# The last stage of a four-layer convolution kernel: two batches kept on chip, six loaded eight parts ahead

## The chip, the cores and the metric

The kernel runs on one core of a Trainium2 chip. The time is device microseconds of one execution; a measurement is the median of several executions. A profile is one further execution, recorded by the hardware profiler, whose span runs from its first to its last instruction. Engines are named as in the profile: PE (matrix multiply, with PEld for its weight loads), DVE (vector), ACT (scalar, activation functions), POOL (GpSimd), SP (the engine that issues most transfers). A queue's name with a q (SPq, ACTq) is the engine's instruction sequencer, which issues transfers.

## What is computed

The input is 8 batches of 128 channels and 64 x 64 points in float32. Four layers follow each other, each added to its own input after a group norm:

```
x = x + L0(gn(x))     # a state-space scan beside a 3x3 convolution
x = x + L1(gn(x))     # four directional passes over rows and columns
x = x + L2(gn(x))     # gated convolutions; its result is x3
x = x + L3(gn(x))     # deformable convolution, then a norm over the whole batch
```

Only the end of layer 3 matters here. With `out` the deformable convolution with its bias:

```
mu  = out.mean(axis=(0, 2, 3), keepdims=True)
var = out.var(axis=(0, 2, 3), keepdims=True)
out = (out - mu) * rsqrt(var + 1e-05)
out = out * gamma + beta
y   = x3 + where(out >= 0, out, 0.1 * out)
```

The mean and the variance run over all batches and points of a channel, so no point of the result can be finished before the last batch of the deformable convolution is done.

## The kernel before

A batch is 4096 columns on 128 partitions (channels); most work goes in parts of T = 512 columns, NCH = 8 to a batch. Layer 0 and the first half of layer 1 run first. Then a hand-written order (under `tc.manual_schedule()`, where instructions are issued in the order of the program) interleaves layer 1's second half, layer 2 and layer 3 in steps called ticks, N = 96 to a batch: at tick n, layer 3 works on batch n // N - 1 while layer 2 works on the batch after it. `spread(thread, steps, first, last)` divides a thread of small actions evenly over a range of ticks. The last 96 ticks hold layer 3 of batch 7 alone.

Layer 3 (class `Layer3`), a tick: `gather` (L1158) lets POOL issue three indirect DMAs, each fetching 128 rows of 512 values out of a table in HBM; ACT and DVE weigh and add the four corners (L1184, L1189, L1200 to L1202), PE turns the tile (`turn`, L1209), ACT copies it (L1219), PE multiplies with the weights (L1227). `biased` (L1233) adds the bias into a tile `o_out` of 512 columns, and `store` (L1242) has SP send it to `od` in HBM and DVE take its statistics (L1244). The gathered tiles are six buffers of the tag `got`. From tick L1R on, when layer 1 is done, they are ten slots of 1536 columns cut out of X instead, a tile of 4096 x 4 values for each partition (16384 columns) that held layer 1's state; `got` is then no longer used.

Layer 2 (class `Layer2`) writes x3 to `x3d` in HBM (L947) and uses tiles of the tags x2, xn2, t1, t3, tok (two buffers each) and x3h (one). For the last batch it ends some 14 ticks before tick 8N; its last transfers on SP are the table stores of L999.

The end stage is `finish` (L1255), called after the pools of layers 2 and 3 and the manual schedule are closed (L145). It derives mean and scale from the statistics (L1264 to L1268), opens a pool of four buffers, and goes over 32 parts of E = 1024 columns, four to a batch: SP loads x3 (L1274) and the stored result (L1276), DVE subtracts the mean and multiplies (L1277), ACT adds beta (L1278), DVE takes the larger of a value and its tenth (L1279), POOL adds x3 (L1280), ACT issues the store (L1281). A load into a buffer waits for the store out of it four parts earlier.

Of the kernel before, what the change touches and what calls it, by code (L numbers as in the profile page):

```python
# [10 lines left out]
F32 = mybir.dt.float32  # L11
I32 = mybir.dt.int32
AF = mybir.ActivationFunctionType
ALU = mybir.AluOpType
# [3 lines left out]
P = 128  # L18
B, C, H, W = 8, 128, 64, 64
HW = H * W  # L20
# [13 lines left out]
@with_exitstack  # L34
def conv_preact_kernel(ctx: ExitStack, tc: tile.TileContext, a: dict, out: bass.AP):
    nc = tc.nc
    x_in = a["x"].rearrange("b c h w -> b c (h w)")
    y_out = out.rearrange("b c h w -> b c (h w)")

    const = ctx.enter_context(tc.tile_pool(name="const", bufs=1))  # L40
    dram = ctx.enter_context(tc.tile_pool(name="dram", bufs=1, space=DRAM))


    ident = const.tile([P, P], F32, name="ident")
    make_identity(nc, ident)

    gmat = const.tile([P, P], F32, name="gmat")
    nc.gpsimd.memset(gmat, 0.25)
    gview = gmat.rearrange("p (g q) -> p g q", q=4)
    nc.gpsimd.affine_select(  # L50
        out=gview, in_=gview, pattern=[[-4, 32], [0, 4]], compare_op=ALU.is_ge,
        fill=0.0, base=0, channel_multiplier=1,
    )
    nc.gpsimd.affine_select(
        out=gview, in_=gview, pattern=[[4, 32], [0, 4]], compare_op=ALU.is_ge,
        fill=0.0, base=3, channel_multiplier=-1,
    )
    eps = const.tile([P, 1], F32, name="eps")
    nc.gpsimd.memset(eps, 1e-5)

    x1d = [dram.tile([C, HW], F32, name=f"x1d{b}") for b in range(B)]
    x2d = [dram.tile([C, HW], F32, name=f"x2d{b}") for b in range(B)]
    od = [dram.tile([C, HW], F32, name=f"od{b}") for b in range(B)]
    x3d = [dram.tile([C, HW], F32, name=f"x3d{b}") for b in range(B)]
    tables = [dram.tile([SIDE * SX, 2 * C], F32, name=f"table{b}") for b in range(B)]

    bcd = [dram.tile([P // 2, T], F32, name=f"bcd{i}") for i in range(2)]


    norm1 = const.tile([P, B, 2], F32, name="norm1")  # L70

    A, Z = range(NB2), range(NB2, B)
    norm2 = const.tile([P, B, 2], F32, name="norm2")
    st = const.tile([P, B * NCH, 6], F32, name="bn_st")
    xp = ctx.enter_context(tc.tile_pool(name="x", bufs=1))
    w1 = ctx.enter_context(tc.tile_pool(name="l1", bufs=2))
    X = xp.tile([P, HW, NB2], F32, name="X")
    layer0(tc, a, ident, gmat, x_in, x1d, bcd, norm1, Layer1First(tc, a, w1, x1d, norm1, X))  # L80

    with tc.tile_pool(name="l2w", bufs=1) as wp, tc.tile_pool(name="l2", bufs=2) as w2, tc.tile_pool(
        name="l3", bufs=2
    ) as w3, tc.tile_pool(name="l12ps", bufs=1, space=PSUM) as p2, tc.tile_pool(
        name="l3ps", bufs=2, space=PSUM
    ) as p3, tc.tile_pool(name="l3pr", bufs=1, space=PSUM) as pr, tc.manual_schedule():
        bank = p2.tile([P, T], F32, name="ps_l1")
        ps_l1 = bank[:, 0 : W * NB2].rearrange("p (w b) -> p w b", b=NB2)
        add = lambda tiles, ahead, b: residual(
            tc, w1, tiles, ahead, bank, gmat, eps, x1d, x2d, X, [(i, b[i]) for i in range(NB2)], norm2  # L90
        )


        first = add(lambda: w3.tile([P, Layer3.G3 * 4 * C], F32, tag="got", name="x_got", bufs=6), 4, A)
        for _ in range(NCH):
            next(first)
        two = Layer2(tc, a, ident, gmat, eps, x2d, x3d, tables, norm2, wp, w2, p2)
        three = Layer3(tc, a, ident, tables, od, st, wp, w3, p3, pr, X.rearrange("p n b -> p (n b)"))


        N = two.TICKS
        plans = {}
        for b in range(B):
            for when, what in two.plan(b).items():
                plans.setdefault(b * N + when, []).extend(what)
        ahead = []

        def spread(thread, steps, first, last):

            ahead.append((thread, steps, first, last))  # L110

        spread(first, 3 * NCH, 0, 12)
        for i in range(NB2):
            spread(load_x(tc, w1, x1d, norm1, X, i, Z[i]), NCH + 1, 4 * i, 4 * i + 4)

        n_l1 = 4 * (H - 1)
        L1A, L1Z = 18, NB2 * N - 22
        early = N - L1A
        L1R = L1Z + 40
        spread(add(lambda: w1.tile([P, T], F32, name="x1", bufs=3), 1, Z), NB2 * NCH, L1Z, L1R)  # L120
        step = propagate(tc, a, w1, ps_l1, X)
        next(step)
        taken = {}
        for n in range(min(plans), (B + 1) * N):
            b, i = n // N - 1, n % N
            if n < N:
                l1 = n >= L1A
            else:
                l1 = [(min(m, L1Z) - N) * (n_l1 - early) // (L1Z - N) for m in (n, n + 1)]
                l1 = l1[1] - l1[0]  # L130
            if l1:
                next(step)
            if b >= 0:
                three.tick(b, i, two.done, 1, n >= L1R)
            if l1:
                next(step)
            for f in plans.pop(n, ()):
                f()
            for k, (thread, steps, first, last) in enumerate(ahead):
                while first <= n and taken.get(k, 0) < -(-steps * min(n + 1 - first, last - first) // (last - first)):  # L140
                    taken[k] = taken.get(k, 0) + 1
                    next(thread)
        while three.late:
            three.tick()
    finish(tc, a, eps, od, x3d, y_out, st, const)  # L145


def layer0(tc, a, ident, gmat, x_in, x1d, bcd, norm1, layer1):
# [975 lines left out]
        return events  # L1124


class Layer3:


    PAIR, G3, WT = 2, 3, 4  # L1130

    def __init__(self, tc, a, ident, tables, od, st, wp, w2, pp, pr_pool, more):
        nc = self.nc = tc.nc
        self.ident, self.tables, self.od, self.st = ident, tables, od, st
        self.w2, self.pp, self.more = w2, pp, more
        self.dcn_w = wp.tile([P, KK, P], F32, name="dcn_w")
        nc.sync.dma_start(self.dcn_w, a["dcn_w"])
        self.dcn_b = wp.tile([P, 1], F32, name="dcn_b")
        nc.sync.dma_start(self.dcn_b, a["dcn_b"])

        self.prod = pr_pool.tile([P, 2, T], F32, name="prod")
        self.samp, self.blocks = {}, {}
        self.late = {}
        self.n = 0

# [86 lines left out]

    def biased(self, b, t0, ps):  # L1233
        nc, N2 = self.nc, self.PAIR * P
        if t0 % 4 == 0:
            self.out = self.w2.tile([P, T], F32, name="o_out")
        o = self.out[:, t0 % 4 * P : t0 % 4 * P + N2]
        nc.scalar.activation(o, ps, AF.Identity, bias=self.dcn_b)
        if t0 % 4:
            self.later(2, self.store, b, t0 // 4, self.out)  # L1240

    def store(self, b, g, out):  # L1242
        self.nc.sync.dma_start(self.od[b][:, g * T : (g + 1) * T], out)
        self.nc.vector.bn_stats(self.st[:, b * NCH + g, :], out)  # L1244

    def tick(self, b=None, i=0, done=None, halves=2, more=False):
# [5 lines left out]
        self.n += 1  # L1252


def finish(tc, a, eps, od, x3d, y_out, st, wp):  # L1255

    nc = tc.nc
    E = 2 * T
    gamma = wp.tile([P, 1], F32, name="gamma")
    nc.sync.dma_start(gamma, a["gamma"])  # L1260
    beta = wp.tile([P, 1], F32, name="beta")
    nc.sync.dma_start(beta, a["beta"])
    mv = wp.tile([P, 2], F32, name="bn_mv")
    nc.vector.bn_aggr(mv, st.rearrange("p a s -> p (a s)"))  # L1264
    sc = wp.tile([P, 1], F32, name="bn_sc")
    nc.scalar.activation(sc, mv[:, 1:2], AF.Sqrt, bias=eps)
    nc.vector.reciprocal(sc, sc)
    nc.vector.tensor_mul(sc, sc, gamma)  # L1268
    with tc.tile_pool(name="l3e", bufs=4) as ep:
        for b in range(B):  # L1270
            for g in range(HW // E):
                s = slice(g * E, (g + 1) * E)
                x3 = ep.tile([P, E], F32, name="x3")
                nc.sync.dma_start(x3, x3d[b][:, s])  # L1274
                v = ep.tile([P, E], F32, name="o_in")
                nc.sync.dma_start(v, od[b][:, s])  # L1276
                nc.vector.tensor_scalar(v, v, mv[:, 0:1], sc, ALU.subtract, ALU.mult)  # L1277
                nc.scalar.activation(v, v, AF.Identity, bias=beta)  # L1278
                nc.vector.scalar_tensor_tensor(v, v, 0.1, v, ALU.mult, ALU.max)  # L1279
                nc.gpsimd.tensor_add(x3, x3, v)  # L1280
                nc.scalar.dma_start(y_out[b][:, s], x3)  # L1281


def layouts(i):
# [55 lines left out]
```

## Time and profile before

| what | value |
|---|---|
| time, median of 3 (range) | 7452.86 us (7450.63 to 7460.66) |
| the profiled execution: its own time / its span | 7436.8 us / 7435.1 us |
| granted TensorE clock, mean | 0.857 |
| busy share of the span: PE, DVE, POOL, ACT | 76%, 65%, 55%, 45% |
| last 512 columns of layer 3 (start of L1244) | 7266.15 us |
| first operation of L1277 | 7272.93 us |
| last add of L1280 ends | 7427.85 us |
| moved from 7266 to 7436 | 50.62 MB, 298 GB/s on average |

The busy shares are averages over stages with different limits, so they say little on a stage of 169 us at the end of 7435; that stage has to be read on its own. In lists of groups and of single instructions, a row has the line, the engine, the operation, what is written and read, and the shapes; a bracket at the end says how long the engine had been idle and what ended that. In lists of waits, the columns are the total in us, how many waits, and the longest. "remote" is a releaser that the profile could not name. A row of a table by windows has the busy us of PE, PEld, DVE, ACT and POOL, each with its count, then the granted clock, the busy share of the DMA engines and GB/s.

The transfers of the end stage, issues with their size:

| transfer | issued by | count | KB each |
|---|---|---|---|
| x3 load (L1274) | SP | 32 | 512 |
| result load (L1276) | SP | 32 | 512 |
| output store (L1281) | ACT | 32 | 512 |

### The profile page before, as it was taken

To read this page: it belongs to the slowest core of one execution; us is meant where nothing else is said; L and a number is where in the kernel's file an instruction comes from. 1 tells how busy PE (TensorE), PEld (TensorE's weight loads), DVE (VectorE), ACT (ScalarE), POOL (GpSimd) and SP (SyncE) were. 2 spreads that over 40 slices of the span, in tenths; PEclk is the share of its full clock that TensorE was granted. 3 is DMA by queue.
4 is the path that set the end of the run, shared out by engine and by line. 5 is a ranking of instruction groups with operands and counts; after the bars stand their busy time and mean duration, and the time that the engine had idled before them with its cause. 6 is when DMAs were issued, how large, how long until landed. Compare 5 with 4: busy or idle time off the path is not lost.

```text
span 7435.1 us, 79753 instructions
## 1 busy us (share of the span) xinstructions
PE 5633.9 (76%) x25130; PEld 3374.0 (45%) x25130; DVE 4822.2 (65%) x6334; ACT 3349.0 (45%) x7610; POOL 4120.9 (55%) x3773
## 2 busy tenths in 40 slices
PE   6888888899999999779898988984556565554330
PEld 1222222255556556647676767762333333333220
DVE  4988889666666666230366666758767676776665
ACT  3555655433333332020255555554556565565552
POOL 3878778545545454000255555555666666666664
PEclk9888888799999999989999999996777677776665
DMA  1111111101100100130356666667677666666667
GB/s 57 43 58 54 57 56 53 42 29 34 32 30 30 31 20 18 59 124 24 96 180 188 189 183 180 192 187 243 211 217 219 208 212 209 211 212 201 187 182 272
DMA packets 360134, 935.09 MB, mean 126 GB/s; under 512 B 64168, under 2 KB 99248, under 8 KB 357664
## 3 DMA queue, kind: packets, MB, share of 16 engines
q0 software_dynamic: 184320, 604.13, 26.7%
q1 hardware_dynamic: 170784, 309.09, 12.8%
q10 hardware_dynamic: 4608, 16.78, 0.6%
q8 instruction: 200, 3.28, 0.2%
q14 instruction: 222, 1.82, 0.1%
HBM read 804.35 MB, written 125.40 MB: 125 GB/s over the span
## 4 chain that ended last, share of the span: by engine, by line
PE 56%; ACT 11%; issue 9%; DVE 9%; another core or an unknown queue 7%; DMA 4%; POOL 4%; SPq 0%; POOLq 0%; DVEq 0%; ACTq 0%
PE u_ps L739 13%; PE ps_l L739 11%; ACT X L1184 6%; PE u_ps L575 5%; PE ps_o L1227 5%; PE ps_c L484 3%; PE ps_t L900 3%; PE ps_y L629 3%; PE ps_s L1209 2%; PE ps_x L392 2%; DVE hb L610 2%; POOL hb L621 2%; PE ps_off L1017 2%; PE ps_t L926 1%
## 5 line engine op out<-in xcount | busy, mean ns | idle before, releaser
L1173 POOL DMA_INDIRECT X<-table,idx x1386 | 1317.9, 951 | 717.0 <-issue 276.6
L1173 POOL DMA_INDIRECT got<-table,idx x918 | 885.1, 964 | 1291.2 <-DVE idx L1078 529.6
L621 POOL TENSOR_TENSOR hb<-hb,bc 128x1024 f32<-128x1024 f32 x512 | 1207.1, 2358 | 47.0 <-POOL carry L616 4.5
L610 DVE TENSOR_TENSOR_SCAN hb<-da,carry,u_ps 128x512 f32<-128x512 f32 x896 | 1097.8, 1267 | 76.4 <-PE ps_y L629 19.8
L592 ACT ACTIVATE da<-dt_ps 128x1024 f32<-128x1024 f32 x512 | 524.8, 1025 | 1284.2 <-PE dt_ps L575 1087.4
L1184 ACT ACTIVATE X<-X,wgt 128x128 f32<-128x128 f32 x2772 | 867.5, 396 | 41.5 <-issue 37.7
L1227 PE MATMUL ps_o<-samp,dcn_w 128*128 128x256 f32 x2304 | 711.8, 455 | 182.9 <-issue 95.8
L1219 ACT COPY samp<-ps_s 128x384 f32<-128x384 f32 x768 | 362.9, 473 | 1043.9 <-remote 563.0
L575 PE MATMUL u_ps<-u,m_u 32*128 32x512 f32 x2048 | 652.3, 716 | 131.2 <-DVE hb L610 130.5
L599 DVE TENSOR_TENSOR u_ps<-u_ps,bc 128x1024 f32<-128x1024 f32 x512 | 625.8, 1222 | 191.2 <-PE dt_ps L575 173.9
L1209 PE MATMUL ps_s<-ident,X 128*128 128x128 f32 x1386 | 306.4, 344 | 576.2 <-ACT samp L1219 287.0
L575 PE MATMUL dt_ps<-dt,m_dt 32*128 32x512 f32 x2048 | 664.0, 728 | 31.5 <-ACT da L592 25.7
L1227 PEld LDWEIGHTS ps_o<-samp,dcn_w 128*128 128x128 f32 x2304 | 507.3, 231 | 309.4 <-issue 128.6
L747 DVE SCALAR_TENSOR_TENSOR X<-ps_l,X 128x256 f32<-128x256 f32 x252 | 106.6, 423 | 734.5 <-PE ps_l L739 553.6
L1200 DVE TENSOR_TENSOR prod<-prod,X 128x384 f32<-128x384 f32 x462 | 260.8, 565 | 480.0 <-ACT X L1184 320.5
L1184 ACT ACTIVATE got<-got,wgt 128x128 f32<-128x128 f32 x1836 | 570.3, 393 | 1.1 <-issue 1.1
L1209 PEld LDWEIGHTS ps_s<-ident,X 128*128 128x128 f32 x1386 | 206.1, 176 | 708.9 <-ACT samp L1219 330.5
L616 POOL COPY carry<-hb 128x2 f32<-128x2 f32 x512 | 111.4, 218 | 735.0 <-DVE hb L610 678.8
L1189 DVE TENSOR_TENSOR prod<-X,prod 128x768 f32<-128x768 f32 x462 | 444.5, 962 | 46.2 <-ACT prod L1156 27.6
L747 DVE SCALAR_TENSOR_TENSOR X<-u_ps,X 128x256 f32<-128x256 f32 x252 | 106.9, 424 | 562.7 <-PE u_ps L739 560.4
L900 PE MATMUL ps_t<-xn,w 128*128 128x512 f32 (+4 forms) x688 | 344.8, 656 | 66.5 <-issue 23.0
L575 PEld LDWEIGHTS u_ps<-u,m_u 32*128 32x128 f32 x2048 | 169.6, 202 | 483.6 <-DVE hb L610 282.2
(227 smaller groups left out, 10644.6 us busy)
## 6 DMA issues: line engine op xcount, KB each, us to landing
bc<-bcd SPq DMA_DIRECT2D x512, 64.0 KB
table<-tok SPq DMA_DIRECT2D x128, 256.0 KB
x<-x1d SPq DMA_DIRECT2D x96, 256.0 KB
X<-table,idx POOLq DMA_INDIRECT x1386
x<-x2d SPq DMA_DIRECT2D x48, 384.0 KB
x3h<-x3d SPq DMA_DIRECT2D x16, 1056.0 KB
x_st<-in_x SPq DMA_DIRECT2D x64, 256.0 KB
x_o<-in_x SPq DMA_DIRECT2D x64, 256.0 KB
```

The lines of the kernel that those rows point to most:

```text
L575: nc.tensor.matmul(ps[:, j, :], lhsT=mask[q, r].rearrange("p d n -> p (d n)"), rhs=S[c][src, h][q, :], start=True, stop=True,)
L592: nc.scalar.activation(da, steps[i]["dt"], AF.Exp)
L599: nc.vector.tensor_mul(st["bc"], st["bc"], s["bc", h][:, 0].unsqueeze(1).to_broadcast([P, 2, T]))
L610: nc.vector.tensor_tensor_scan(hb[:, j, :], st["da"][:, j, :], st["bc"][:, j, :], start, ALU.mult, ALU.add)
L621: nc.gpsimd.tensor_mul(hb, hb, S[c]["bc", h][:, 1].unsqueeze(1).to_broadcast([P, 2, T]))
L739: nc.tensor.matmul(ps[:, c0:c1, :], lhsT=w[:, k, :], rhs=v[:, prev, c0 + k - PAD : c1 + k - PAD, :], start=(k == PAD), stop=(k == K - 1),)
L900: nc.tensor.matmul(ps[:, o0 - a0 : o1 - a0, :], lhsT=self.w1[:, k, :], rhs=S["xn", g][:, i0 + o0 : i0 + o1, :], start=(k == 2), stop=(k == 4),
L1173: nc.gpsimd.indirect_dma_start(out=got[:, k, :, :].rearrange("p q c -> p (q c)"), out_offset=None, in_=tab, in_offset=bass.IndirectOffsetO ...
L1184: nc.scalar.activation(got[:, k, q, :], got[:, k, q, :], AF.Identity, scale=wgt[:, t, k0 + k, q : q + 1])
L1189: nc.vector.tensor_mul(prod, got[:, :, 0:2, :], w.unsqueeze(3).to_broadcast([P, G3, 2, C]))
L1209: nc.tensor.transpose(ps[:, k, :], got[:, k, 0, :], self.ident)
L1227: nc.tensor.matmul(ps, lhsT=self.dcn_w[:, k, :], rhs=samp[:, k - k0, :], start=(k == 0), stop=(k == KK - 1))
```

## The change

Batches 6 and 7 (KEEP = 2) no longer go through HBM for the end stage. `biased` writes their result into slices of six tiles of the tag `got`, `store` skips their transfer and keeps the statistics, and a new thread `keep` loads their x3, in 16 transfers of 512 columns, into tiles of layer 2's tags; it is spread over ticks 8N + 8 to 8N + 72.

`finish` is called inside the pools and the manual schedule. The 24 parts of the other six batches are loaded into X, in eight places of 2048 columns (x3 beside the result), and the first eight are asked for before anything else. The end stage first handles the 16 kept parts of 512 columns, then the 24 of 1024. In each step of its loop DVE's L1277 and ACT's L1278 of one part come ahead of DVE's L1279, POOL's add, the store and the next load of the part before it.

```
+        kept = {}
+        spread(two.keep(three.KEEP, kept), three.KEEP * NCH, B * N + 8, B * N + 72)
...
-    finish(tc, a, eps, od, x3d, y_out, st, const)
+        finish(tc, a, eps, od, x3d, y_out, st, const, kept, three.kept, X.rearrange("p n b -> p (n b)"))
...
+    def keep(self, batches, kept):
+
+        room = [(tag, n) for tag, n in (("x2", 1), ("xn2", 1), ("t1", 1), ("t3", 1), ("tok", 2)) for _ in range(2)]
+        todo = [(b, g) for b in range(B - batches, B) for g in range(NCH)]
+        for tag, n in room + [("x3h", 4)]:
+            t = self.w2.tile([P, n * T], F32, tag=tag, name="x3k", bufs=1 if tag == "x3h" else 2)
+            for i in range(n):
+                b, g = todo.pop(0)
+                kept[b, g] = t[:, i * T : (i + 1) * T]
+                self.nc.sync.dma_start(kept[b, g], self.x3d[b][:, g * T : (g + 1) * T])
+                yield
...
     def biased(self, b, t0, ps):
         nc, N2 = self.nc, self.PAIR * P
-        if t0 % 4 == 0:
+        n = (b - B + self.KEEP) * NCH + t0 // 4
+        if t0 % 4 == 0 and n < 0:
             self.out = self.w2.tile([P, T], F32, name="o_out")
+        elif t0 % 4 == 0:
+            if n % 3 == 0:
+                self.place = self.w2.tile([P, self.G3 * 4 * C], F32, tag="got", name="o_kept", bufs=6)
+            self.out = self.kept[b, t0 // 4] = self.place[:, n % 3 * T : (n % 3 + 1) * T]
...
     def store(self, b, g, out):
-        self.nc.sync.dma_start(self.od[b][:, g * T : (g + 1) * T], out)
+        if (b, g) not in self.kept:
+            self.nc.sync.dma_start(self.od[b][:, g * T : (g + 1) * T], out)
         self.nc.vector.bn_stats(self.st[:, b * NCH + g, :], out)
...
-    E = 2 * T
+    E, AHEAD = 2 * T, 8
...
+    todo = [(b, g) for b in range(B) if (b, 0) not in odk for g in range(HW // E)]
+
+    def place(n):
+
+        at = n % AHEAD * 2 * E
+        return room[:, at : at + E], room[:, at + E : at + 2 * E]
+
+    def loads(n):
+        if n < len(todo):
+            b, g = todo[n]
+            for t, d in zip(place(n), (x3d, od)):
+                nc.sync.dma_start(t, d[b][:, g * E : (g + 1) * E])
+
+    for n in range(AHEAD):
+        loads(n)
...
-    with tc.tile_pool(name="l3e", bufs=4) as ep:
-        for b in range(B):
-            for g in range(HW // E):
-                s = slice(g * E, (g + 1) * E)
-                x3 = ep.tile([P, E], F32, name="x3")
-                nc.sync.dma_start(x3, x3d[b][:, s])
-                v = ep.tile([P, E], F32, name="o_in")
-                nc.sync.dma_start(v, od[b][:, s])
-                nc.vector.tensor_scalar(v, v, mv[:, 0:1], sc, ALU.subtract, ALU.mult)
-                nc.scalar.activation(v, v, AF.Identity, bias=beta)
-                nc.vector.scalar_tensor_tensor(v, v, 0.1, v, ALU.mult, ALU.max)
-                nc.gpsimd.tensor_add(x3, x3, v)
-                nc.scalar.dma_start(y_out[b][:, s], x3)
+
+    parts = [(x3k[b, g], odk[b, g], y_out[b][:, g * T : (g + 1) * T]) for b, g in odk]
+    parts += [(*place(n), y_out[b][:, g * E : (g + 1) * E]) for n, (b, g) in enumerate(todo)]
+    for n in range(len(parts) + 1):
+        if n < len(parts):
+            _, v, _ = parts[n]
+            nc.vector.tensor_scalar(v, v, mv[:, 0:1], sc, ALU.subtract, ALU.mult)
+            nc.scalar.activation(v, v, AF.Identity, bias=beta)
+        if n:
+            x3, v, out = parts[n - 1]
+            nc.vector.scalar_tensor_tensor(v, v, 0.1, v, ALU.mult, ALU.max)
+            nc.gpsimd.tensor_add(x3, x3, v)
+            nc.scalar.dma_start(out, x3)
+            if n > len(odk):
+                loads(n - 1 - len(odk) + AHEAD)
```

More of the change, by code (lines that the diff above doesn't have):

```diff
@@ L1124, in plan @@
         return events
+    def keep(self, batches, kept):
[8 more added lines that the diff above has]
+                yield
 class Layer3:
     PAIR, G3, WT = 2, 3, 4
+    KEEP = 2
     def __init__(self, tc, a, ident, tables, od, st, wp, w2, pp, pr_pool, more):
@@ L1141, in __init__ @@
         self.prod = pr_pool.tile([P, 2, T], F32, name="prod")
-        self.samp, self.blocks = {}, {}
+        self.samp, self.blocks, self.kept = {}, {}, {}
         self.late = {}
@@ L1252, in tick, with finish @@
         self.n += 1
-def finish(tc, a, eps, od, x3d, y_out, st, wp):
+def finish(tc, a, eps, od, x3d, y_out, st, wp, x3k, odk, room):
     nc = tc.nc
-    E = 2 * T
+    E, AHEAD = 2 * T, 8
     gamma = wp.tile([P, 1], F32, name="gamma")
```

## The prediction

> **What bounds the kernel now.** I read the granted clock and the slices first (one core, span 7435.1 us, clock 0.857), then the end of the span by windows, its groups with shapes kept apart, who waited for whom, and last single instructions in time. Before the end stage stands layer 3; its last instruction is the statistics of the last 512 columns at 7266.15. The end stage runs from there to 7435.1, 169 us, 2.3% of the span. The columns of the windows are busy us and count per engine, then PE clock, DMA share, GB/s.
>
> ```profile
> 7250.00:7266.00 16.00, 8.72 (x33) 6.45 (x33) 10.65 (x17) 6.66 (x20) 0.00 (x0) 0.68 0.01 2
> ...
> 7269.50:7428.00 158.50, 0.00 (x0) 0.00 (x0) 91.34 (x64) 36.62 (x32) 84.43 (x32) 0.50 0.89 313
> 7428.00:7435.10 7.10, 0.00 (x0) 0.00 (x0) 0.00 (x0) 0.00 (x0) 0.00 (x0) 0.50 0.18 74
> ```
>
> The DMA engines idle while layer 3 drains, then are 89% busy. That looks like a transfer-bound stage. The waits say it is not that alone:
>
> ```profile
> DVE o_in L1277 <- DMA o_in<-od: 33.5, 18, 4.8
> ...
> SPq L1274 <- DMA out<-x: 109.7, 28, 10.0
> ```
>
> SP (the load queue) waits 28 times for a store to land, since the ring has four buffers: a part's load, its arithmetic and its store follow each other, and four of them go round in some 21 us (32 parts in 169 us are 5.28 us each). DVE waits for loads 33.5 us in all. The other 125 us are not DMA. Three parts between such waits show what they are:
>
> ```profile
> 7346.12 0.80 DVE L1277 TENSOR_SCALAR o_in<-o_in,bn_mv,bn_sc 128x1024 f32<-128x1024 f32 x1
> 7346.33 2.79 POOL L1280 TENSOR_TENSOR x<-x,o_in 128x1024 f32<-128x1024 f32 x1 [1.22 <-DVE o_in L1279]
> 7346.96 1.15 ACT L1278 ACTIVATE o_in<-o_in,beta 128x1024 f32<-128x1024 f32 x1 [2.87 <-DVE o_in L1277]
> 7348.14 2.07 DVE L1279 SCALAR_TENSOR_TENSOR o_in<-o_in 128x1024 f32<-128x1024 f32 x1 [1.22 <-ACT o_in L1278]
> ...
> 7350.13 0.80 DVE L1277 TENSOR_SCALAR o_in<-o_in,bn_mv,bn_sc 128x1024 f32<-128x1024 f32 x1
> 7350.34 2.79 POOL L1280 TENSOR_TENSOR x<-x,o_in 128x1024 f32<-128x1024 f32 x1 [1.22 <-DVE o_in L1279]
> ```
>
> The DVE op of L1279, 1.22 us where POOL is idle, takes 2.07 when it starts inside POOL's add, and ends 1.09 us after that add (7350.21 against 7349.12). At 7311.78 the op of L1277, else 0.81, takes 2.92 beside an add and ends 0.55 after it. POOL's add, 2.34 alone, takes 2.79 when a DVE op is in the way. So the two engines take turns: 0.55 + 1.09 + 2.34 = 3.98 us a part, and the period shown (7346.12 to 7350.13) is 4.01. Of 154.9 us from the first DVE op (7272.93) to the end of the last add (7427.85), 32 x 4.01 = 128.3 are this alternation, the remaining 26.6 filling and loads.
>
> Layer 3's last two batches, where the change also puts its hands:
>
> ```profile
> ACT samp L1219 <- remote: 171.3, 15, 12.6
> ...
> q14 instruction: 15, 0.12, 0.1%
> ```
>
> In the last 400 us ACT stands still 15 times for some 11 us, while queue 14 moves 15 packets in about the same time (6900 to 7260). Each stall I followed ends about 3.2 us after POOL's last gather before it (7230.6 to 7233.84). POOL issues gathers at one per 1.25 us and is never held by SP.
>
> **What the Trainium skill says.** "GPSIMD Engine Reference", section 1 (Specifications), puts the SBUF interfaces as shared with VectorE, with contention against DVE instructions in a 2-port perf mode or with two SBUF inputs. L1277 (one SBUF tensor, 1024 elements in 0.81 us) and L1279 (two inputs) fit both clauses, and the trace agrees: 2.07 against 1.22. "DMA: Bandwidth & Descriptors", Issuing engines are not separate DMA queues: loads by SP and stores by ACT run on the same 16 engines and interleave; the DMA shares of up to 0.97 in 7300 to 7320, with both in flight, agree. "CRC Debugging", Comparing the Two Runs, names queue 14 as the refill of the sequencers' instructions; the 15 stalls beside 15 packets agree, though that they are the same events is my inference.
>
> **The change, part by part.** Sums are against the profiled execution (span 7435.1, its time 7436.8). The median shown is 7452.86, 16 above; I carry the difference over.
>
> 1. *Start of the end stage.* The scale is ready at 7269.48 (L1268 starts 7269.32, 0.16). Now the first DVE op waits for its load until 7272.93. With the first 16 parts on chip it starts at 7269.5. Two short DVE ops and an ACT op of 0.68 (a 128x512 ACTIVATE, L936 row) before the first op of L1279: about 7270.7.
> 2. *Sixteen kept parts of 512 columns.* POOL's 128x512 add is 1.27 (the L439, L441 and L468 rows, 1270 to 1274 ns). The two DVE shares halve to 0.27 and 0.54; with 0.07 for handing over: 2.15 each, 34.4 in all, where eight parts of 1024 took 32.1. Halving the width costs 2.3.
> 3. *Twenty-four loaded parts.* 24 x 4.01 = 96.2 if no load is late. The new order puts L1277 of the next part ahead of L1279 on DVE and the store behind the next ACT op. Behind the store, which waits for POOL, stands ACT's next op, and DVE waits for that: 0.34 + 1.15 after an add ends, under the 2.34 of the following add. So that wait is covered; if POOL had no add ready it would cost 1.5 a part.
> 4. *Sum.* 7270.7 + 34.4 + 96.2 - 0.5 (two DVE ops already done) = 7400.8 for the last add. The last store and the end take 7.25 now (7427.85 to 7435.1) and stay: 7408.0, that is -27.1.
> 5. *Are loads in time?* SP no longer waits for closing pools. Gathers use ten slots of 1536 columns of X; the first load needs slots 0 and 1, last turned by PE seven steps before the end, at about 7244. Others follow to 7263, all 8.4 MB landing near 7275, while the first is needed at 7305. From there a part asks 1.57 MB in 4.01 us, 392 GB/s, more than the 352 of the best 20 us. But eight parts are ahead: until the last load lands 16 loads and 16 stores (25.2 MB) must move, 85 us at the old mean of 298, so 7390, and it is needed at 7305 + 23 x 4.01 = 7397. Late loads cost nothing above about 280 GB/s. The DMA idle shown in 7250 to 7266 is used, but it does not set the end.
> 6. *Layer 3, batch 6 on.* Sixteen stores of 256 KB leave SP. With them gone nothing on SP holds the sixteen x3 loads: SP runs past its last table store (issued by 6768.7) straight into them, so 4.2 MB come as a burst near 6770, earlier than their place in the order suggests. SP then stops at the X loads; nothing else is behind it. The table's buffers there were done by then, so there is no new wait for them. The burst lies beside gathers (DMA share 0.88 and 0.63 in 6770 to 6790). Bounds: -2 (the stores removed make room) to +12 (4.2 MB at 350 GB/s, all of it delaying gathers). The ten slots cover most; I take +1.
> 7. *Preloads beside the drain.* They fill the DMA engines while PE and ACT finish. An instruction refill at that point can be held: 0 to 10.5 (one stall of the kind shown). The refill before it ends with the gathers, so I take +1.
>
> Total -25: span 7410, median 7427.9.
>
> **Rivals.** *Faster: the turns are not what decides.* If the new order let DVE and POOL overlap more, transfers would bind: 16 loads and 24 stores after 7305, 29.4 MB at 350 GB/s, 84 us, end at 7393: -42, 7411. For it: adds and DVE ops overlap in layer 0. Against it: those there read PSUM, and every stretched op above. 12%. *Late loads:* at 240 to 250 GB/s the 25.2 MB take 103 us, the last part starts 11 us late, and the gain shrinks to about 13: 7440. For it: single stretches of 4 us moved only 210 to 264 (7286, 7294, 7322). Against: the waits of the ring lie in them. 10%. *Layer 3 pays for the burst* in full, 12 of item 6: 7440. 10%. *Slower: instruction refills starve behind the new traffic.* The burst and then the preloads keep the engines full in places where ACT needs its refills; price 10.5 to 12.6 a stall (the remote row). It decides from three added stalls on the path that ends layer 3: 3 x 11.4 = 34 against 27, so +7, 7460. For it: refills stop while gathers run. Against it: the end stage itself runs at 0.89 DMA share without one stall of that size on ACT. 6%. The change doing what it says is hardly in doubt.
>
> **How the numbers follow.** The likeliest case, 62%, is -25 with its own range -35 to -17. Eight times in 10 the time should lie in 7403 to 7445: this leaves out the slower rival and the outer half of the small gains and of the large one. A measurement of this kernel tells 0.2%, 15 us, from no change. The likeliest case and the faster rival lie beyond it, of the two small gains about a third: 0.79 faster, 0.15 within, 0.06 slower.
>
> **What would show it.** Right: the first DVE op of the end within 0.5 us of the scale; kept parts every 2.1 to 2.2 us; loaded ones every 4.0 with POOL's add stretched or DVE's ops stretched, and almost no DVE wait for o_in loads; the last add near 7401; X loads from about 7244; x3 loads in a burst near 6770; layer 3's end within 3 us of 7266. Wrong: DVE waits for loads above 5 us in all, a loaded part under 3.7 us, or layer 3 ending after 7275.

## The result and the profile after

| kernel | median us (range, runs) | ratio to before, 95% interval |
|---|---|---|
| before | 7458.44 (7450.63 to 7467.47, 6) | |
| changed | 7428.00 (7421.59 to 7438.23, 6) | 0.9960 (0.9947 to 0.9973) |

The change takes 30.4 us off the median. The two profiled executions differ by only 4.2 us in span (7435.1 and 7430.9), and before anything is read from them it has to be seen where that comes from. Layer 3's statistics give 64 marks along both, one for each part of 512 columns (starts of L1244 before, of L1269 after):

| statistics of part | before | after | difference |
|---|---|---|---|
| 25 (batch 3 begins) | 5228.4 | 5228.4 | 0.0 |
| 41 (batch 5 begins) | 6083.0 | 6092.3 | +9.3 |
| 49 (batch 6, first that the change touches) | 6507.6 | 6521.5 | +13.9 |
| 63 | 7241.6 | 7264.1 | +22.5 |
| 64, the last | 7266.1 | 7289.2 | +23.0 |
| end of the span, from the last statistics | 168.9 | 141.7 | -27.2 |

Up to the start of batch 3 the two stay within 7 us of each other; from there the changed one falls behind evenly, first over three batches in which both kernels have the same instructions. The execution that was profiled before took 7436.8 us, less than any of the six timed ones. And had layer 3 lost 23 us in every execution, the median would have gained some 4 us, not 30. So the 23 us are looked at as a difference between executions (the first experiment tests that), and the end stage is compared from its own start, the last statistics.

The end stage of the changed kernel by windows; columns are busy us and count of PE, PEld, DVE, ACT and POOL, then PE clock, DMA share, GB/s:

```profile
7292.50:7328.00 35.50, 0.00 (x0) 0.00 (x0) 32.62 (x36) 12.59 (x17) 23.85 (x16) 0.51 0.41 158
...
7350.00:7370.00 20.00, 0.00 (x0) 0.00 (x0) 20.00 (x11) 5.73 (x6) 14.19 (x6) 0.50 0.97 361
7370.00:7390.00 20.00, 0.00 (x0) 0.00 (x0) 20.00 (x11) 5.73 (x6) 14.19 (x6) 0.50 1.01 401
...
7424.00:7431.00 7.00, 0.00 (x0) 0.00 (x0) 0.00 (x0) 0.00 (x0) 0.00 (x0) 0.50 0.19 75
```

The kept parts (first row) leave the DMA engines 41% busy. In the loaded parts DVE has no idle moment, and from 7350 to 7390 the DMA engines are full as well. About half of DVE's full share is standing still, as single instructions show:

```profile
7357.62 0.80 DVE L1315 TENSOR_SCALAR X<-X,bn_mv,bn_sc 128x1024 f32<-128x1024 f32 x1
7357.78 2.84 POOL L1320 TENSOR_TENSOR X<-X 128x1024 f32<-128x1024 f32 x1 [1.16 <-DVE X L1319]
7358.34 3.36 DVE L1319 SCALAR_TENSOR_TENSOR X<-X 128x1024 f32<-128x1024 f32 x1
...
7361.62 0.80 DVE L1315 TENSOR_SCALAR X<-X,bn_mv,bn_sc 128x1024 f32<-128x1024 f32 x1
7361.78 2.84 POOL L1320 TENSOR_TENSOR X<-X 128x1024 f32<-128x1024 f32 x1 [1.16 <-DVE X L1319]
```

A loaded part comes every 4.00 us. DVE's second operation starts at 7358.34, in the middle of POOL's add, which ends at 7360.62, and itself ends 1.08 after that: 3.36 us for work of 1.22. With the 0.80 of the first operation that is 2.02 us of work in a period of 4.00. Before, these turns were broken 15 to 18 times by waits for loads; now they run on without a gap.

### The profile page after: what moved, and what is told of

It reads as the page before. It is cut to its first block, busy times and chain, and to the rows that moved or that the text cites. A ratio compares the mean times of both kernels' runs of the same rounds, so it can differ in the third digit from the quotient of the medians.

```text
span 7430.9 us, 79727 instructions
## 1 busy us (share of the span) xinstructions
PE 5644.5 (76%) x25130; PEld 3377.1 (45%) x25130; DVE 4854.7 (65%) x6350; ACT 3346.5 (45%) x7618; POOL 4120.3 (55%) x3781
## 4 chain that ended last, share of the span: by engine, by line
PE 55%; ACT 13%; issue 9%; DVE 8%; another core or an unknown queue 8%; POOL 4%; DMA 3%; SPq 0%; DVEq 0%; POOLq 0%; ACTq 0%
PE u_ps L743 13%; PE ps_l L743 11%; ACT X L1203 7%; PE u_ps L579 5%; PE ps_o L1246 4%; PE ps_c L488 3%; PE ps_t L904 3%; PE ps_y L633 3%; PE ps_s L1228 2%; PE ps_x L396 2%; DVE hb L614 2%; PE ps_off L1021 2%; POOL hb L625 2%; PE ps_t L930 1%
## 5 line engine op out<-in xcount | busy, mean ns | idle before, releaser
L1219 DVE TENSOR_TENSOR prod<-prod,X 128x384 f32<-128x384 f32 x462 | 260.8, 565 | 491.4 <-ACT X L1203 308.9
```

## The experiments

Most of them ran on other chips of the same kind, where the kernel before takes 7002 to 7006 us instead of some 7455. Each is compared with the kernel before on its own chip; the run with the stores by POOL had one of the slower chips. The end stage differs less between chips (168.9 and 167.5 us before, 141.7 on both after). "End stage" is the time from the start of the last statistics to the end of the span, in the profiled execution.

| kernel | median us | kernel before there | ratio, 95% interval | end stage us |
|---|---|---|---|---|
| before, again | 7004.28 (one) | 7002.40 | | 167.5 |
| changed, again | 6979.40 (one) | 7002.40 | | 141.7 |
| eight buffers | 6977.81 | 7002.40 | 0.9962 (0.9948 to 0.9975) | 144.6 |
| none kept | 6983.37 | 7002.40 | 0.9974 (0.9963 to 0.9984) | 149.1 |
| four ahead | 7011.69 | 7006.15 | 1.0010 (1.0002 to 1.0019) | 174.5 |
| four ahead, stores by SP | 7046.93 | 7005.74 | 1.0057 (1.0043 to 1.0070) | 207.4 |
| four ahead, stores by POOL | 7459.97 | 7450.77 | 1.0008 (0.9997 to 1.0018) | 166.9 |
| loads held | 6974.99 | 7005.74 | 0.9959 (0.9945 to 0.9972) | 141.7 |
| add on DVE | 6962.10 | 7006.15 | 0.9940 (0.9927 to 0.9954) | 118.0 |
| add on DVE, one ACT operation | 6953.10 | 7006.15 | 0.9927 (0.9913 to 0.9940) | 108.5 |
| the same, parts mixed | 6944.26 | 7006.15 | 0.9917 (0.9903 to 0.9930) | 104.8 |
| eight buffers, add on DVE, one ACT operation | 6963.93 | 7005.74 | 0.9939 (0.9925 to 0.9952) | 129.2 |

**Does the change slow layer 3?** Both kernels were profiled again, on one chip, with no edit.

> The kernel before, profiled once more. In the two profiles so far layer 3's last statistics start at 7266.15 before and 7289.19 after, 23 us later, and the distance grows evenly from batch 3 on, ahead of any instruction that the change touches. If the change costs layer 3 these 23 us, this profile ends layer 3 within 3 us of 7266. If they are a difference between executions, the end of layer 3 lies anywhere between 7260 and 7300. Either way the end stage takes 169 us, within 3.

> The changed kernel, profiled once more. If the change costs layer 3 some 23 us, its last statistics start within 3 us of 7289. If that was a difference between executions, they lie within the spread of the kernel before on the same chip. The end stage takes 141.7 us again, within 1, as DVE and POOL taking turns set it: 2.13 a kept part, 4.01 a loaded one.

The last statistics start at 6835.1 before and at 6836.0 after. On a chip that is faster as a whole the marks at 7266 and 7289 mean nothing, and of the 23 us, 0.9 are left. At the 63rd statistics the changed kernel is even 2.9 us ahead. The end stage is 141.7 us again, to the tenth. So the 23 us were in the main a difference between executions.

The faster chip shows none of the "remote" waits that fill layer 3 on the first one, so the first pair has to answer for itself whether these grew. In batches 3 to 5, ahead of anything the change touches, ACT had 51 of them before and 67 after (259 and 298 us); from the 49th statistics to the last, 35 and 34 (237 and 234 us). In that last stretch the changed kernel's profile falls back by another 9.1 us, at the rate of the batches ahead of it (13.9 over 24 parts, 9.1 over 15), though DVE's waits for unnamed releasers are 85 us there in place of 34. The run with the stores by POOL, on a chip of that speed, ends layer 3 late as well, at 7291. With one profile of the kernel before on such a chip, a price of a few us there is neither shown nor excluded.

One thing in layer 3 is the change's: from the 63rd to the 64th statistics the kernel before takes 29.2 us there, the changed one 33.0. Who waited for whom in those last 34 us, before and then after:

```profile
DVE prod L1189 <- DMA X<-table,idx: 5.8, 7, 1.6
```

```profile
DVE prod L1208 <- DMA X<-table,idx: 8.0, 6, 2.9
```

The last gathers are waited for longer, and SP's loads into X now move beside them. The other profiles on faster chips agree: with such loads the stretch took 32.3 to 35.4 us in six, without them 28.3 to 29.9 in four. On the first chip it took 24.5 and 25.1, so there it cost 0.6.

**Depth, or bytes kept on chip?** First the kernel before, with one number changed:

```
-    with tc.tile_pool(name="l3e", bufs=4) as ep:
+    with tc.tile_pool(name="l3e", bufs=8) as ep:
```

> The kernel before with eight buffers in its last pool instead of four, and nothing else. If depth of loading is what the change gains by, and the turns of DVE and POOL are the next bound: 6.8 us until the first DVE operation, 2.3 of filling, 32 x 4.01 = 128.3, then 7.25: 144.6 from the last statistics to the end, that is 24 us under the kernel before. If the 8.4 MB kept on chip are what gains, transfers stay the bound and the time stays within 5 us of the kernel before.

The end stage took 144.6 us, the number expected. One wait of DVE for a load is left, the first:

```profile
DVE o_in L1277 <- DMA o_in<-od: 3.9, 1, 3.9
```

```profile
6910.00:6930.00 20.00, 0.00 (x0) 0.00 (x0) 13.92 (x11) 5.74 (x5) 13.96 (x5) 0.50 1.02 401
```

The DMA engines are full here too, at 401 GB/s, where a part every 4.01 us asks for 392; that DVE waits for a load only once says that the turns set the pace, and the last run below, with the same loads and no turns, takes 129.2. So four more buffers bring nearly all that the whole change brings. All its other parts make 144.6 into 141.7, which is about the earlier start of the first DVE operation (3.4 us after the statistics against 7.2).

Then the changed kernel with no batch kept:

```
-    KEEP = 2
+    KEEP = 0
```

> The changed kernel with no batch kept on chip (KEEP = 0): all 32 parts are loaded into X, eight ahead. By the turns: 5.4 us to the first operation of the second DVE line, 32 x 4.01 = 128.3, 7.25, less 0.6: 140.4 from the last statistics to the end, so within 2 us of the changed kernel's 141.7, and a time within 5 us of it. By the bytes: 8.4 MB more to move, 21 us at 400 GB/s and 28 at 298, so a time near the kernel before.

The loss against the changed kernel is 7.4 us of end stage: more than the 2 us that the turns allowed and far less than the bytes would cost. SP's issues show what had been left out of the expectation:

```profile
6801.71 37.48 SPq L1268 DMA_DIRECT2D od<-o_out  x2
6839.24 1.62 SPq L1285 DMA_DIRECT2D gamma<-in_gamma  x1
6840.91 0.42 SPq L1287 DMA_DIRECT2D beta<-in_beta  x1
6841.51 0.33 SPq L1299 DMA_DIRECT2D X<-x3d  x1
```

With nothing kept, layer 3's last stores stand ahead of the loads on SP, so the first load goes out at 6841.51, after the last statistics at 6838.9, and the arithmetic starts late. The first operation of L1319 in the changed kernel, 4.7 us after its last statistics, and here, 12.3 us after:

```profile
7293.90 0.69 DVE L1319 SCALAR_TENSOR_TENSOR o_kept<-o_kept 128x512 f32<-128x512 f32 x1 [0.33 <-ACT o_kept L1316]
```

```profile
6851.17 1.22 DVE L1319 SCALAR_TENSOR_TENSOR X<-X 128x1024 f32<-128x1024 f32 x1
```

From there to the last operation of L1319 it is 124.3 us in the changed kernel and 124.2 here, so the late start is the whole loss. DVE waits for loads again in most parts:

```profile
DVE X L1315 <- DMA X<-od: 36.4, 25, 4.2
```

But a part still comes every 4.1 us: DVE waits for a load in part of the time that it would have stood behind POOL's add. Keeping two batches is thus worth a little, as it clears SP's queue and gives the engines work while the first loads run.

Then depth from the other side:

```
-    E, AHEAD = 2 * T, 8
+    E, AHEAD = 2 * T, 4
```

> The changed kernel with loads four parts ahead instead of eight (AHEAD = 4), two batches kept. By depth: the ring of four gives back the 5.28 us a part of the kernel before, but for the first four, which are there: 20 x 1.27 = 25 us lost, a time within 6 us of the kernel before. If keeping two batches on chip and the early start are what gains, at most 8 us are lost against the changed kernel.

With four ahead and two batches kept the end stage loses 32.8 us (25 were expected) and the kernel is 5.5 us slower than before, at 8.4 MB less to move after layer 3. Depth carries the change.

That it came out slower than the old ring of four points to the new order of the loop:

```profile
6928.35 2.34 POOL L1320 TENSOR_TENSOR X<-X 128x1024 f32<-128x1024 f32 x1 [1.76 <-DVE X L1319]
...
6933.50 0.81 DVE L1315 TENSOR_SCALAR X<-X,bn_mv,bn_sc 128x1024 f32<-128x1024 f32 x1 [5.23 <-DMA X<-od]
6934.23 1.22 DVE L1319 SCALAR_TENSOR_TENSOR X<-X 128x1024 f32<-128x1024 f32 x1
6934.35 1.15 ACT L1316 ACTIVATE X<-X,beta 128x1024 f32<-128x1024 f32 x1 [6.03 <-DVE X L1315]
...
6935.52 2.34 POOL L1320 TENSOR_TENSOR X<-X 128x1024 f32<-128x1024 f32 x1 [4.84 <-DVE X L1319]
```

The first operation of a part waits 5.23 us for its load, and the second operation of the part before, which needs only data already there, stands behind it on DVE. POOL's add waits for that, the store for the add, a later load for the store. Two attempts to take this apart followed; both finish a part before they begin the next.

```
+        if n:
+            x3, v, out = parts[n - 1]
+            nc.vector.scalar_tensor_tensor(v, v, 0.1, v, ALU.mult, ALU.max)
+            nc.gpsimd.tensor_add(x3, x3, v)
+            nc.sync.dma_start(out, x3)
+            if n > len(odk):
+                loads(n - 1 - len(odk) + AHEAD)
         if n < len(parts):
             _, v, _ = parts[n]
...
```

> As the one with loads four ahead, but a part's second DVE operation, add and store are issued before the next part's first operations, and SP issues the stores. With four ahead a first operation that waits for its load held the previous part's second operation, its add and store, and so the load behind that store. If that is why four ahead came out slower than the kernel before, the end stage falls from 174.5 to some 150 to 160 us. If four buffers as such cost this, it stays within 4 us of 174.5.

This failed: 207.4 us. A store on SP now stands behind loads that wait for the store before it to land, so one part goes round at a time, every 7.6 us:

```profile
6952.76 0.81 DVE L1322 TENSOR_SCALAR X<-X,bn_mv,bn_sc 128x1024 f32<-128x1024 f32 x1 [4.33 <-DMA X<-od]
...
6960.34 0.81 DVE L1322 TENSOR_SCALAR X<-X,bn_mv,bn_sc 128x1024 f32<-128x1024 f32 x1 [4.33 <-DMA X<-od]
```

The edit had moved the obstruction, not removed it. With the store on POOL (`nc.gpsimd.dma_start(out, x3)` in its place):

> As the one with loads four ahead and the part before finished first, but POOL issues the stores, behind its add. On SP a store stood behind loads that waited for the store before it, so only one part went round at a time (7.57 us a part). Here neither a late load nor such a load holds a store. If the order of waits cost the first variant with four ahead its time, the end stage is 150 to 165 us; if four buffers as such do, it stays within 4 us of that variant's 174.5.

166.9 us lies just outside the first band and well off the second: 7.6 us of the 174.5 went, and DVE's waits for loads fell from 70.5 to 23.7 us. The store's path differs too (POOL instead of ACT issues it): 2.7 of the 7.6 us lie behind the last add, which the order doesn't touch, so some 5 are left for the order. The rest, 25.2 over 141.7, is near the 22.9 that four buffers in place of eight cost the kernel before. The chip is another one, so this splits the loss only roughly, and the whole kernel's time is not told from that of the kernel before.

**Is the early start into X worth its price?** In the changed kernel a transfer that needs the last statistics was put ahead of the loads:

```
+    nc.sync.dma_start(od[B - 1][:, 0:6], st[:, B * NCH - 1, :])
     for n in range(AHEAD):
         loads(n)
```

> The changed kernel with the first X loads held until layer 3's last statistics: a transfer of six values for each partition out of those statistics is put ahead of them on SP. If loading into X while layer 3 drains delays the last gathers (profiles of kernels with such loads took 33.0 to 35.5 us from the 63rd to the 64th statistics, those without 28.2 to 29.5), that stretch is back at 29 and the time 2 to 5 us under the changed kernel, as the first loaded part is wanted only some 37 us into the end stage, which stays at 141.7. If the early start is worth something, the end stage grows by up to 10 us.

The end stage is 141.7 again: loading before layer 3's end buys nothing, as 16 kept parts cover the loads. The stretch between the last two statistics was 31.0, half of the way back to 29; what the other half is stays open. The changed kernel wasn't timed on that chip, so whether its time falls by holding the loads stays open.

**Do DVE and POOL really take turns?** The add of the changed kernel was given to DVE:

```
-            nc.gpsimd.tensor_add(x3, x3, v)
+            nc.vector.tensor_add(x3, x3, v)
```

> The changed kernel with the last add on DVE instead of POOL, nothing else. If the two engines take turns, DVE alone needs 0.55 + 1.09 + 1.1 and some 0.15 between, 2.9 us a loaded part and 1.6 a kept one, against 4.01 and 2.13; the kept parts end 8 us sooner, then 36 MB less what went before at the 400 GB/s seen at DMA share 1.0 bind at some 4 us a part once the eight loaded ahead are used up: 8 to 16 us under the changed kernel. If POOL worked beside DVE, this would be slower than the changed kernel.

Groups with shapes kept apart (busy us and mean ns of one behind the bar), first of the changed kernel, then of this one:

```profile
L1319 DVE SCALAR_TENSOR_TENSOR X<-X 128x1024 f32<-128x1024 f32 x24 | 78.7, 3279 | 0.8 <-ACT X L1316 0.8
L1320 POOL TENSOR_TENSOR X<-X 128x1024 f32<-128x1024 f32 x24 | 66.8, 2785 | 28.2 <-DVE X L1319 25.8 <-issue 1.2 <-DMA out<-X 1.2
```

```profile
L1320 DVE TENSOR_TENSOR X<-X 128x1024 f32<-128x1024 f32 x24 | 29.4, 1225 | 0.8
L1319 DVE SCALAR_TENSOR_TENSOR X<-X 128x1024 f32<-128x1024 f32 x24 | 29.3, 1220 | 4.7 <-ACT X L1316 4.7
```

One engine with all three operations is 23.7 us quicker in the end stage than the two together. The operation of L1319 takes 1220 ns without POOL and 3279 with it. This is the run that shows the turns. A kept part comes every 1.78 us here in place of 2.13, a loaded one every 3.12 and, once loads are waited for, every 3.75; 3.5 of the 23.7 us lie behind the last add, which had not been foreseen and whose cause is open.

**What binds when the turns are gone?** ACT's operation can multiply as well as add, so the subtraction and the scale move into it:

```
+    shift = wp.tile([P, 1], F32, name="bn_shift")
+    nc.vector.scalar_tensor_tensor(shift, mv[:, 0:1], -1.0, sc, ALU.mult, ALU.mult)
+    nc.vector.tensor_add(shift, shift, beta)
...
-            nc.vector.tensor_scalar(v, v, mv[:, 0:1], sc, ALU.subtract, ALU.mult)
-            nc.scalar.activation(v, v, AF.Identity, bias=beta)
+            nc.scalar.activation(v, v, AF.Identity, bias=shift, scale=sc)
```

> As the one with the add on DVE, and the subtraction and scale moved into ACT's one operation (scale and bias both per channel), so that DVE has two operations a part: 2.3 us a loaded part, 1.3 a kept one. ACT needs 1.15. Transfers bind from the ninth loaded part on: 13 us saved on the kept parts against the changed kernel, little more on the loaded ones, 12 to 22 us under it.

108.5 us, 33 under the changed kernel where 12 to 22 were expected. With the parts mixed as well:

```
...
+    parts = []
+    while far or near:
+        parts += far[:3] + near[:2]
+        far, near = far[3:], near[2:]
...
```

> As the one with ACT's single operation and two on DVE, and the kept parts spread among the loaded ones, two after each three, so that transfers never pause: after the last statistics 42 MB less the 8.4 loaded before, 33.6 MB at 400 GB/s, 84 us, with 5 at the start and 10 at the end: 99 against 141.7, some 40 us under the changed kernel, if transfers are then the bound. If DVE and ACT still bind, as for the one before.

104.8 us, where 99 were expected; the time is 61.9 us under the kernel before, about twice the gain of the change. Its end stage by windows:

```profile
6838.00:6874.00 36.00, 0.00 (x0) 0.00 (x0) 29.20 (x32) 16.29 (x16) 0.00 (x0) 0.55 0.91 347
6874.00:6896.00 22.00, 0.00 (x0) 0.00 (x0) 17.73 (x19) 8.53 (x8) 0.00 (x0) 0.50 1.01 376
6896.00:6916.00 20.00, 0.00 (x0) 0.00 (x0) 12.38 (x13) 7.18 (x7) 0.00 (x0) 0.50 1.01 382
6916.00:6936.00 20.00, 0.00 (x0) 0.00 (x0) 18.99 (x21) 10.69 (x10) 0.00 (x0) 0.50 0.80 309
```

The DMA engines are over 90% busy from the start to 6916, where the changed kernel left them 41% busy for 35 us, and DVE has time to spare: there transfers bind. In the last 20 us before the end DVE is full again and they are not. The last run asks what the kept bytes are worth then, with the kernel before, eight buffers, and the same arithmetic:

> The kernel before with eight buffers, ACT's single scale-and-bias operation and the last add on DVE; nothing kept on chip. With the turns gone, 50.3 MB at 400 GB/s are 126 us, with 3 before and 7 behind: 136 from the last statistics to the end against 144.6 with eight buffers alone. So the bytes kept on chip, worth nothing beside the turns, are worth some 30 us here, against the mixed order with two batches kept (104.8). If bytes do not bind even then, it comes within 10 us of the mixed order.

129.2 us, where 136 were expected, against 104.8 with two batches kept. So what the change has beside its depth is worth 24 us here, and was worth 3 beside the turns. These 24 us are not the kept bytes alone: the mixed order is worth 3.7 of them, and of the 50.6 MB that moved after the last statistics in this run the mixed one moved 36.0, since 8.4 MB were kept and some 6 were loaded before layer 3 ended. The two were not tried apart.

## Why the prediction was right, step by step

The predicted 7428 is the measured median, but part of that is luck: the median of before rose from 7452.86 to 7458.44 with three more runs, so the gain was 30.4 us (by the interval, 20 to 40) where 25 were forecast. The end stage, which carries the forecast, came out as the sum had it; the 2 us that were set against it for layer 3 are below what these medians can tell. One sign named as wrong did come: layer 3's profile ended at 7289, after 7275. The sign was too narrow: executions of the kernel before alone lie between 7436.8 and 7467.5 us.

- *Start.* Said: first DVE operation within 0.5 us of the scale, 3.35 us after the last statistics. Measured: 3.37.
- *Kept parts.* Said 2.15 each. Measured: 2.13 (7298.76 to 7300.89).
- *Loaded parts.* Said 4.01 each with no late load. Measured: 4.00, and DVE waited for none.
- *Sum.* The last add was to end 134.7 us after the last statistics; it ended at 134.5. The end stage was to lose 27.1 us; it lost 27.2. The last 7.25 us stayed 7.25.
- *Loads in time.* Right, with little to spare: counted by the packets of SP's queue, loads landed an estimated 6 to 7 us before their part from the twelfth on, where the step left 7 for the last. The rates at full share, 361 to 401 GB/s, are well above the 298 that the step used and close to the 392 that the turns ask for. A faster pair of engines would soon have met the transfers, as the run with the add on DVE shows: its loaded parts slow down from 3.12 to 3.75 us.
- *The burst.* SP issued the sixteen x3 loads from 6786.50 on within 20 us, one behind the other, right after the last table store, as foreseen (near 6770 was said; in this profile layer 3 was 17 us late by then):

```profile
6754.62 31.82 SPq L1003 DMA_DIRECT2D table<-tok  x8
6786.50 20.14 SPq L1140 DMA_DIRECT2D x3k<-x3d  x16
```

  On the faster chips no price can be told: from the 49th to the 63rd statistics the seven profiles with the burst took 621.9 to 624.1 us, the four without it 620.5 to 623.3. On the first chip it is not separated from the drift.
- *Preloads beside the drain.* The place was right and the mechanism was not. A held instruction refill was expected; neither of the first two profiles has a "remote" wait of ACT in that stretch, and on the faster chip the last gathers were waited for longer. The term was 1 us and measured 0.6 on the first chip, 3.8 on the other.
- *The rivals.* Overlap of DVE and POOL: refuted by the period of 4.00 and by the run with the add on DVE. Late loads: none here, but real at four ahead, where the order of the loop makes them worse. Layer 3 paying 12 for the burst: not seen. Refills starving behind the new traffic: the 23 us in the first pair of profiles looked like it, but ACT's waits grew only ahead of that traffic.

What the prediction did not say is that the change's largest edits are not what gains most. Its own account, that the turns bind as soon as loads are in time, implied that eight buffers alone would do nearly as much, as they did.

## What to carry to other kernels

When a stage looks bound by transfers, work out what its engines need once transfers are in time; here that sum gave the gain to a few tenths, and showed that saved bytes would stay unused until DVE and POOL no longer stood in each other's way. Remove the binding thing first (here the add on POOL), then the bytes: kept batches, early loads and their order together were worth 3 us before that and 24 after. A loop that issues the next part's first operation ahead of the last part's remaining ones is safe only while loads are hardly late, since an engine that takes its instructions in order passes a wait on to everything behind it: waits of 1.5 us a part cost next to nothing with eight ahead, waits of over 5 us did harm with four.

## What the runs showed of the hardware

- DVE and POOL excluded each other almost wholly in these operations. Of DVE's 0.81 and 1.22 us, 0.55 and 1.09 were left to do when POOL's add of 2.34 ended; the three make 3.98 us, against a period of 4.00 to 4.01.
- Chips of one kind differed by 6% on the same kernel, 7002.4 us against 7458.4. Of the 431 us between the two profiles' last statistics all but 9 arise after the first ones (3737.4 and 3728.3), that is in layer 3's stretch, and there the slower chip's ACT waits on "remote", 563.0 us on line L1219 alone. In the faster chip's profile no engine has such a wait, though queue 14 moved packets there as well (20 in 6400 to 6800, against 15 in 360 us). There the gathers' landing is waited for instead:

```profile
ACT X L1184 <- DMA X<-table,idx: 110.6, 196, 1.9
```

  That these waits make up much of the difference is likely, not shown. If queue 14's packets are the refills, as the prediction inferred, a refill does not have to stall. Why ACT stalls on one chip and not on another was not tried.
- Loads and stores together moved up to 420 GB/s over 20 us (the run with the add on DVE), against at most 364 in the kernel before (7297.5 to 7317.5).
